# A fourth buffer for the scan's states, and the next sequence's softplus in the buffer of u

## The chip, the cores and the metric

The kernel runs on one core of one Trainium2 chip. The metric is the device time of one execution in microseconds. The engines are called by their names in the profile: PE (TensorE, matmuls), PEld (its weight loads), DVE (VectorE), ACT (ScalarE), POOL (GpSimd), SP (SyncE, whose queue issues the DMAs named here). Each engine runs its own instructions strictly in order.

## What is computed

The input is x, 16 sequences of 512 tokens with 256 features, float32. Four residual layers follow one another:

```
x = x + mamba(layernorm(x))         # the state-space scan: the part that changes here
x = x + ffn(layernorm(x))           # "f": weights and activations rounded to FP4 in blocks of 16
x = x + linear_attention(layernorm(x))
x = x + ffn(layernorm(x))           # "g": the same weights
```

The scan layer, with 16 states per feature:

```
x_in = x @ w_in                                   # u
dt   = softplus(x_in @ w_x[:, :64] @ w_dt + b_dt) * 0.099 + 0.001
B, C = columns 64..79 and 80..95 of x_in @ w_x
bar  = exp(dt * A),  A = -exp(A_log)
h    = bar * h + inp,   inp[n] = B[n] * sum_d dt[d] A[d, n] u[d]
y    = sum_n h[:, n] C[n] + D * u
```

## The kernel before

All 16 sequences pass through four stages: scan, ffn "f", attention, ffn "g". The stages of different sequences overlap: `run_all` holds a generator for each stage with a begin and a length in units of a sequence's scan, and always advances the one that is furthest behind. A generator yields estimated costs between its pieces. From this the program text is emitted in one interleaved order, and the tile framework's scheduler then arranges each engine's instructions. The resulting order on each engine is fixed before the kernel runs. Stage b of the scan begins at b, of "f" at b+1, of attention at b+2.1, of "g" at b+3.1, so in the middle of the run four sequences are in flight.

A sequence's scan (`mamba`) has 16 steps, one for each (e, j, q0), a tile of 128 rows (16 states times 8 features) by 2x512 times:

1. `spread` (L520) copies rows of softplus's result from the DRAM tile `dd` to one of four decay tiles `bars`, each feature row to its 16 state rows. It can be issued when the scan that used this tile four steps earlier has ended.
2. `decay` (L527, L530) turns it into the decay: two Exp on ACT and one Square.
3. L548 is the scan on DVE, h = bar * h + inp, over 1024 columns. L552 multiplies by C (`cm`).
4. Two steps make a pair: L558 on PE sums the 16 states of both into `py`.

`h` has the tag "hs" with three buffers, so a scan has to wait until the py matmul three scans earlier has read its tile. `py` begins with the product of D's diagonal and u (L544); the second of a sequence's two py tiles begins at step 9, where `halfway` is set. After the eighth and the sixteenth step py goes through L565 (yT), transposes (L568) and L571 into the residual x.

The scan of sequence b+1 needs a `prologue` (L449), which is woven between the steps of scan b:

- `front` (L435): layer norm statistics and the transposed, scaled input tT_m;
- pz (L457), softplus's argument, on PE; L466 and L467 on ACT take its absolute value and its ReLU; L471 and L472 are Tanh and Ln with a table load; L473 on DVE joins them to dt;
- eight DMAs (L478) that write dt to `dd`;
- pcm and its copy cm (L483);
- a guard, which holds the generator until scan b has passed its half; it is needed because u has one buffer and u of sequence b is read by the second L544;
- pu and its two copies to u (L490), L493 (dt times u, DVE), pg and pbm on PE (L496, L457), L501 (ACT), L502 (DVE), which gives `term`.

The next `mamba` then copies `term` to the two halves of `inp` (L510 on ACT, L511 on POOL), which has one buffer, so these wait for the sixteenth scan of the sequence before; then its first scan can start.

The other names in the prediction: in an ffn, `hidden(c)` runs pg and pu (L605), Tanh (L611), two products on DVE (L612, L613), and the FP4 rounding (L230 to L252, with one ACT step L248, big); `down(c)` runs transposes pt_h (L627), copies hqT (L631, L636), the matmul po (L640) and the residual (L377 or L647). In the attention, `scores` makes psc (L722) and the masked sm (L729), and `attend` makes pn (L745, L753), pr, pk, pkv, and yT (L773); pro (L800) is its projection. `h_g_3` means chunk 3 (of 0 to 3) of "g", and so on. PSUM has seven banks for all of these and one for py.

Of the kernel before, what the change touches and what calls it, by code (L numbers as in the profile page):

```python
# [10 lines left out]
F32 = mybir.dt.float32  # L11
# [6 lines left out]
P = 128  # L18
# [14 lines left out]
def kernel(  # L33
# [19 lines left out]
    B, S, D = x.shape  # L53
# [6 lines left out]
    ND = D // P  # L60
# [18 lines left out]
    def bank(name):  # L79
        return ps.tile([P, 512], F32, tag="bank", name=name)  # L80
# [7 lines left out]
    one = ctx.enter_context(tc.tile_pool(name="one", bufs=1))  # L88
# [8 lines left out]
    begun, turned, stats, halfway = {}, {}, {}, [0]  # L97
# [270 lines left out]
    def summed(i, name):  # L368

        sums = small.tile([P, NC], F32, tag=f"sum{i}", name=f"sum_{name}")  # L370
        dist = small.tile([P, NC], F32, tag=f"dist{i}", name=f"dist_{name}")
        return sums, dist
# [10 lines left out]
    def distances(xt, c, sums, dist):  # L383
        nc.scalar.activation(
            squares, xt[:, c, :], AF.Square, bias=sums[:, c : c + 1], scale=-float(D),
            accum_out=dist[:, c : c + 1],
        )
# [47 lines left out]
    def front(b, xt):  # L435

        stats = small.tile(
            [P, NC, nc.vector.BN_STATS_DIM], F32, tag="stats", name=f"st_m{b}"
        )
        mv = small.tile([P, NC, nc.vector.BN_AGGR_DIM], F32, tag="mv", name=f"mv_m{b}")  # L440
        for c in range(NC):
            nc.vector.bn_stats(stats[:, c, :], xt[:, c, :])
            nc.vector.bn_aggr(mv[:, c, :], stats[:, c, :])
        rstd = inverse(2, mv[:, :, 1], 1.0, f"m{b}")
        yield 2.4
        turned[b] = to_features(one, xt, f"m{b}", rstd)
        yield 1

    def prologue(b, xt):  # L449

        yield from front(b, xt)
        xnT = turned.pop(b)

        def from_xn(w, name):
            p = bank(f"{name}_{b}")
            for k in range(ND):
                nc.tensor.matmul(p, w[:, k], xnT[:, k, :], start=(k == 0), stop=(k == ND - 1))  # L457
            return p

        soft = one.tile([P, ND, S], F32, tag="soft", name=f"soft_{b}")
        dt = one.tile([P, ND, S], F32, tag="dt", name=f"dt_{b}")
        for e in range(ND):
            pz = from_xn(w_z_sb[:, :, ts(e, P)], f"pz{e}")
            nc.scalar.activation(soft[:, e, :], pz, AF.Abs, bias=b_dt_sb[:, e : e + 1])  # L466
            nc.scalar.activation(  # L467
                dt[:, e, :], pz, AF.Relu, bias=b_relu[:, e : e + 1], scale=DT_MAX - DT_MIN
            )
        yield 0.5  # L470
        nc.scalar.activation(soft, soft, AF.Tanh, scale=0.5)  # L471
        nc.scalar.activation(soft, soft, AF.Ln, bias=half_c, scale=0.5 * LN_C)  # L472
        nc.vector.scalar_tensor_tensor(dt, soft, DT_MIN - DT_MAX, dt, ALU.mult, ALU.add)  # L473

        dd = dram.tile([ND, 2, 32, 2, S], F32, tag="dt", name=f"dd_{b}")
        for e in range(ND):
            for q in range(4):
                nc.sync.dma_start(  # L478
                    dd[e, q // 2, :, q % 2, :], dt[32 * q : 32 * q + 32, e, :]
                )  # L480
        yield 1.5
        cm = one.tile([P, S], F32, tag="cm", name=f"cm_{b}", bufs=2)
        nc.scalar.copy(cm, from_xn(w_c_sb, "pcm"))  # L483
        yield 0.1

        while halfway[0] < b:
            yield 0
        u = one.tile([P, ND, S], F32, tag="u", name=f"u_{b}")
        for e in range(ND):
            nc.scalar.copy(u[:, e, :], from_xn(w_in_sb[:, :, ts(e, P)], f"pu{e}"))  # L490
        yield 0.5

        nc.vector.tensor_tensor(dt, dt, u, ALU.mult)  # L493
        pg = bank(f"pg_{b}")
        for k in range(ND):
            nc.tensor.matmul(  # L496
                pg, a_rep[:, k].rearrange("p n i -> p (n i)"), dt[:, k, :],
                start=(k == 0), stop=(k == ND - 1),
            )
        term = dt[:, 0, :]  # L500
        nc.scalar.copy(term, from_xn(w_b_sb, "pbm"))  # L501
        nc.vector.tensor_tensor(term, term, pg, ALU.mult)  # L502
        begun[b] = (u, dd, term, cm)
        yield 2

    def mamba(b, xt):
        u, dd, term, cm = begun.pop(b)

        inp = one.tile([P, 2, S], F32, tag="inp", name=f"inp_{b}")
        nc.scalar.copy(inp[:, 0, :], term)  # L510
        nc.gpsimd.tensor_copy(inp[:, 1, :], term)  # L511

        halves = small.tile([P, ND, NC], F32, tag="halves", name=f"halves_{b}")

        def spread(e, j, q0):

            bar = bars[state["bar"] % NBAR]
            state["bar"] += 1
            src = dd[e, q0 // 2, j * G8 : (j + 1) * G8, :, 1:S]
            nc.sync.dma_start(bar[:, :, 1:S], src.unsqueeze(0).to_broadcast([NS, G8, 2, S - 1]))  # L520
            return bar

        def decay(bar, e, j, q0):

            for i in range(2):
                g = 16 * e + 4 * (q0 + i) + j
                nc.scalar.activation(  # L527
                    bar[:, i, 1:S], bar[:, i, 1:S], AF.Exp, scale=a_col[:, g : g + 1]
                )
            nc.scalar.activation(bar[:, :, 1:S], bar[:, :, 1:S], AF.Square)  # L530
            return bar

        steps = [(e, j, q0) for e in range(ND) for j in range(4) for q0 in (0, 2)]
        sps = [spread(*steps[at]) for at in range(NBAR - 1)]
        ahead = decay(sps[0], *steps[0])
        for at, (e, j, q0) in enumerate(steps):
            bar = ahead
            if at + 1 < len(steps):
                ahead = decay(sps[at + 1], *steps[at + 1])
            if at + NBAR - 1 < len(steps):  # L540
                sps.append(spread(*steps[at + NBAR - 1]))
            if j == 0 and q0 == 0:
                py = ps_y.tile([P, S], F32, tag="y", name=f"py_{b}_{e}")
                nc.tensor.matmul(py, d_diag[:, e], u[:, e, :], start=True, stop=False)  # L544
                if e == ND - 1:
                    halfway[0] = b + 1
            h = one.tile([P, 2, S], F32, tag="hs", name=f"h_{b}_{e}_{j}_{q0}", bufs=3)
            nc.vector.tensor_tensor_scan(  # L548
                h.rearrange("p i t -> p (i t)"), bar.rearrange("p i t -> p (i t)"),
                inp.rearrange("p i t -> p (i t)"), 0.0, ALU.mult, ALU.add,  # L550
            )
            nc.vector.tensor_tensor(h, h, cm.unsqueeze(1).to_broadcast([P, 2, S]), ALU.mult)  # L552
            if q0 == 0:
                h0 = h
            else:

                for q in range(4):
                    nc.tensor.matmul(  # L558
                        py[32 * q : 32 * q + 32, :], red[:, j, :], (h0, h)[q // 2][:, q % 2, :],
                        start=False, stop=(j == 3),  # L560
                    )
            if j == 3 and q0 == 2:

                yT = one.tile([P, S], F32, tag="yT", name=f"yT_{b}_{e}")
                nc.scalar.copy(yT, py)  # L565
                pt = bank(f"pt_y_{b}_{e}")
                for c in range(NC):
                    nc.tensor.transpose(pt[:, ts(c, P)], yT[:, ts(c, P)], ident)  # L568
                for c in range(NC):
                    xc = xt[:, c, ts(e, P)]  # L570
                    nc.vector.scalar_tensor_tensor(  # L571
                        xc, pt[:, ts(c, P)], 1.0, xc, ALU.mult, ALU.add,
                        accum_out=halves[:, e, c : c + 1],
                    )
            yield 3.5

        stats["f", b] = sums, dist = summed(0, f"f{b}")
        nc.vector.tensor_tensor(sums, halves[:, 0, :], halves[:, 1, :], ALU.add)
        for c in range(NC):
            distances(xt, c, sums, dist)  # L580
        yield 2
# [268 lines left out]
    def scan(b):  # L850

        if b + 1 < B:
            xs.append(load(b + 1))
            yield from weave(mamba(b, xs[b]), prologue(b + 1, xs[b + 1]), 1)
        else:
            yield from mamba(b, xs[b])
# [76 lines left out]
```

## Time and profile before

| | us |
|---|---|
| three runs, median (lowest to highest) | 2812.1 (2811.1 to 2816.2) |
| profiled execution, its own time | 2810.3 |
| its span, first to last instruction | 2808.6 |
| PE busy | 2443.9 |
| DVE busy | 2432.7 |
| ACT busy | 1491.0 |
| POOL busy | 171.8 |
| mean granted PE clock | 0.944 of full |

The span is the time from the first to the last instruction on the core. A busy time is the sum of an engine's instructions without the overlap of consecutive ones. A row of the costliest groups gives line, engine, operation, output and inputs, the number of instructions, their total and mean time, and how long the engine was idle just before them, with what ended that. In the answers on waits the three numbers are the total in us, how often, and the longest. In a timeline the two numbers ahead are the start in us from the span's start and the duration; the bracket holds the idle time before and its cause.

Single rows used later: L511 on POOL takes 0.61 to 1.60 us, median 1.46; L478 issues in 0.42 us (median) and lands 1.7 us after; a spread (511 KB) lands 4.7 us after its issue; an ACT table load takes 1.28 us, and there are 33.

### The profile page before, as it was taken

The numbers are of one execution on the slowest core, as the hardware profiler recorded it, in microseconds if no ns is written. First come the engines' busy times: TensorE is split into PE (matmuls) and PEld (weight loads), VectorE is DVE, ScalarE is ACT, GpSimd is POOL, SyncE is SP. The second block draws the span as 40 slices with busy tenths as digits, with TensorE's granted clock in tenths as the row PEclk, the third lists the DMA queues.
The fourth block names the chain that finished last, engine by engine and source line by source line (L and its number), as shares of the span: only waits on it lengthen the run. The fifth ranks groups of instructions, "written<-read, shape, count | busy, mean of one in ns | idle before, by whom it ended". The sixth has DMA issues, their size and how long they took to land.

```text
span 2808.6 us, 34278 instructions
## 1 busy us (share of the span) xinstructions
PE 2443.9 (87%) x12907; PEld 1436.5 (51%) x12907; DVE 2432.7 (87%) x3689; ACT 1491.0 (53%) x2846; POOL 171.8 (6%) x171
## 2 busy tenths in 40 slices
PE   5677889799888898989889898989989898899996
PEld 3234545455555555555555555555555555455664
DVE  7898888898899889989989989898899988987665
ACT  4766564465636456464555646455564645433321
POOL 2000000000001000000100000010000001000000
PEclk7788999999999999999999999999999999999998
DMA  5433212223113131311313222131321312200000
GB/s 141 128 97 83 67 46 53 68 53 83 53 38 83 38 90 38 90 46 38 84 44 79 49 61 74 38 75 45 83 53 51 85 37 69 53 1 8 8 1 15
DMA packets 97146, 165.01 MB, mean 59 GB/s; under 512 B 8434, under 2 KB 92372, under 8 KB 96980
## 3 DMA queue, kind: packets, MB, share of 16 engines
q1 hardware_dynamic: 95360, 161.77, 22.5%
q8 instruction: 101, 1.65, 0.3%
q10 hardware_dynamic: 1620, 1.06, 0.1%
q14 instruction: 65, 0.53, 0.1%
HBM read 146.02 MB, written 16.78 MB: 58 GB/s over the span
## 4 chain that ended last, share of the span: by engine, by line
DVE 40%; PE 35%; DMA 10%; ACT 9%; issue 4%; POOL 2%; SPq 0%; POOLq 0%; ACTq 0%; DVEq 0%
DVE h L548 15%; DMA bar<-dd 10%; PE pg_g L605 5%; DVE h L552 4%; PE pu_g L605 4%; PE po_g L640 3%; PE pg_f L605 3%; PE pu_f L605 3%; PE py L558 3%; ACT bar L527 2%; DVE sm L729 2%; PE pz L457 2%; DVE v_f L244 1%; ACT bar L530 1%; PE po_f L640 1%
## 5 line engine op out<-in xcount | busy, mean ns | idle before, releaser
L548 DVE TENSOR_TENSOR_SCAN h<-bar,inp 128x1024 f32<-128x1024 f32 x256 | 579.6, 2278 | 12.1 <-PE py L558 5.9
L527 ACT ACTIVATE bar<-bar,a_col 128x511 f32<-128x511 f32 x512 | 352.4, 716 | 358.5 <-DMA bar<-dd 305.8
L558 PE MATMUL py<-h,red 128*32 128x512 f32 x1024 | 289.6, 649 | 122.5 <-DVE h L552 121.7
L552 DVE TENSOR_TENSOR h<-h,cm 128x1024 f32<-128x1024 f32 x256 | 311.3, 1218 | 0.6
L530 ACT ACTIVATE bar<-bar 128x1022 f32<-128x1022 f32 x256 | 269.3, 1052 | 3.0
L640 PE MATMUL po_g<-wdT,hqT_g 128*128 128x256 f32 (+1 forms) x768 | 205.9, 412 | 40.2 <-ACT hqT_g L631 40.2
L640 PE MATMUL po_f<-wdT,hqT_f 128*128 128x256 f32 (+1 forms) x768 | 197.9, 400 | 9.5 <-ACT hqT_f L631 8.3
L640 PEld LDWEIGHTS po_g<-wdT,hqT_g 128*128 128x128 f32 (+1 forms) x768 | 143.7, 199 | 113.7 <-ACT hqT_g L631 64.2
L605 PE MATMUL pg_g<-wgT,tT_g 128*128 128x352 f32 x512 | 194.1, 500 | 0.2 <-ACT tT_g L419 0.2
L605 PE MATMUL pu_g<-wuT,tT_g 128*128 128x352 f32 x512 | 185.6, 487 | 0.0
L640 PEld LDWEIGHTS po_f<-wdT,hqT_f 128*128 128x128 f32 (+1 forms) x768 | 137.0, 191 | 95.0 <-ACT hqT_f L636 29.9
L605 PE MATMUL pg_f<-wgT,tT_f 128*128 128x352 f32 x512 | 182.0, 479 | 0.1
L605 PE MATMUL pu_f<-wuT,tT_f 128*128 128x352 f32 x512 | 172.9, 460 | 3.3 <-DVE sm L729 3.3
L729 DVE TENSOR_TENSOR sm<-psc,causal 128x512 f32<-128x512 f32 x256 | 164.1, 680 | 2.2 <-PE pn L753 1.3
L611 ACT ACTIVATE h_g<-pg_g 128x352 f32<-128x352 f32 x128 | 59.1, 462 | 199.9 <-PE pg_g L605 199.9
L558 PEld LDWEIGHTS py<-h,red 128*32 128x32 f32 x1024 | 37.9, 111 | 224.9 <-DVE h L552 173.9
L605 PEld LDWEIGHTS pu_g<-wuT,tT_g 128*128 128x128 f32 x512 | 105.1, 206 | 64.1 <-issue 14.8
L612 DVE SCALAR_TENSOR_TENSOR h_g<-h_g,pg_g 128x352 f32<-128x352 f32 x128 | 65.6, 512 | 79.9 <-ACT h_g L611 78.7
L763 POOL COPY dx<-den 128x256 f32<-128x256 f32 x64 | 42.7, 667 | 1455.7 <-PE pr L768 776.7
L605 PEld LDWEIGHTS pg_f<-wgT,tT_f 128*128 128x128 f32 x512 | 95.4, 195 | 67.4 <-issue 22.8
L678 PE MATMUL pqk<-tT_a,w_qkv_sb 128*128 128x512 f32 x256 | 121.2, 610 | 7.2 <-ACT tT_a L430 7.2
L605 PEld LDWEIGHTS pu_f<-wuT,tT_f 128*128 128x128 f32 x512 | 97.1, 190 | 58.9 <-DVE sm L729 5.2
(237 smaller groups left out, 4674.1 us busy)
## 6 DMA issues: line engine op xcount, KB each, us to landing
bar<-dd SPq DMA_DIRECT2D x256, 511.0 KB, 4.7
x<-in_L_attn_a_x_dram SPq DMA_DIRECT2D x16, 512.0 KB, 4.5
dd<-dt SPq DMA_DIRECT2D x128, 64.0 KB, 1.7
out_dram<-x SPq DMA_DIRECT2D x16, 512.0 KB, 4.9
w_qkv_sb<-in_L_attn_b_W_attn_dram ACTq DMA_DIRECT2D x1, 768.0 KB, 7.3
raw_d<-in_L_ffn_w_down_dram SPq DMA_DIRECT2D x1, 704.0 KB
raw_g<-in_L_ffn_w_gate_dram SPq DMA_DIRECT2D x1, 640.0 KB, 7.1
raw_u<-in_L_ffn_w_up_dram SPq DMA_DIRECT2D x1, 640.0 KB, 6.3
```

The source lines that it names most:

```text
L457: nc.tensor.matmul(p, w[:, k], xnT[:, k, :], start=(k == 0), stop=(k == ND - 1))
L527: nc.scalar.activation(bar[:, i, 1:S], bar[:, i, 1:S], AF.Exp, scale=a_col[:, g : g + 1])
L530: nc.scalar.activation(bar[:, :, 1:S], bar[:, :, 1:S], AF.Square)
L548: nc.vector.tensor_tensor_scan(h.rearrange("p i t -> p (i t)"), bar.rearrange("p i t -> p (i t)"), inp.rearrange("p i t -> p (i t)"), 0.0, ...
L552: nc.vector.tensor_tensor(h, h, cm.unsqueeze(1).to_broadcast([P, 2, S]), ALU.mult)
L558: nc.tensor.matmul(py[32 * q : 32 * q + 32, :], red[:, j, :], (h0, h)[q // 2][:, q % 2, :], start=False, stop=(j == 3),)
L605: nc.tensor.matmul(pw[:, :HF], xqT[:, k, ts(c, P)], wT[:, k, cols], start=(k == 0), stop=(k == ND - 1),)
L611: nc.scalar.activation(hc, pg[:, :HF], AF.Tanh, scale=0.5)
L612: nc.vector.scalar_tensor_tensor(hc, hc, 1.0, pg[:, :HF], ALU.add, ALU.mult)
L640: nc.tensor.matmul(po[:, :D], hqT[:rows, r, :], wdT[:rows, r, :], start=(r == 0), stop=(r == NR - 1),)
L678: nc.tensor.matmul(pz, w_qkv_sb[:, k, ts(je, P)], xnT[:, k, :], start=(k == 0), stop=(k == ND - 1),)
L729: nc.vector.tensor_tensor(t, psc[g].rearrange("p (s t) -> p s t", t=P), causal.unsqueeze(1).to_broadcast([P, NH // 4, P]), ALU.mult,)
```

## The change

The prologue's softplus result `soft` no longer has a buffer of its own: it takes the one of u (tag "u"). The guard moves from before u to before `soft`, since the buffer is free only when scan b has read its own u for the last time. So pz, softplus, the writes to `dd` and cm are issued after the half of scan b, as u was already. The 4 KB per partition that soft held go to a fourth buffer for the states h.

```diff
@@ prologue
+        while halfway[0] < b:
+            yield 0
+
-        soft = one.tile([P, ND, S], F32, tag="soft", name=f"soft_{b}")
+        soft = one.tile([P, ND, S], F32, tag="u", name=f"soft_{b}")
         dt = one.tile([P, ND, S], F32, tag="dt", name=f"dt_{b}")
...
         nc.scalar.copy(cm, from_xn(w_c_sb, "pcm"))
         yield 0.1
-
-        while halfway[0] < b:
-            yield 0
         u = one.tile([P, ND, S], F32, tag="u", name=f"u_{b}")
@@ mamba
-            h = one.tile([P, 2, S], F32, tag="hs", name=f"h_{b}_{e}_{j}_{q0}", bufs=3)
+            h = one.tile([P, 2, S], F32, tag="hs", name=f"h_{b}_{e}_{j}_{q0}", bufs=4)
```

In the changed kernel the lines below the guard's new place are three higher as far as cm (L473 becomes L476); from u on (L490) they are the same.

## The prediction

> **What bounds the kernel now.** I read the page's first part, then the chain, then who VectorE (DVE) waits for, all of it and in one sequence, and last the timelines of that sequence.
>
> ```profile
> span 2808.6 us, 34278 instructions
> PE 2443.9 (87%) x12907; PEld 1436.5 (51%) x12907; DVE 2432.7 (87%) x3689; ACT 1491.0 (53%) x2846; POOL 171.8 (6%) x171
> DVE 40%; PE 35%; DMA 10%; ACT 9%; issue 4%; POOL 2%; SPq 0%; POOLq 0%; ACTq 0%; DVEq 0%
> L548 DVE TENSOR_TENSOR_SCAN h<-bar,inp 128x1024 f32<-128x1024 f32 x256 | 579.6, 2278 | 12.1 <-PE py L558 5.9
> ```
>
> DVE and TensorE (PE) are both near full and share the chain, so the instruction order, above all DVE's, sets the time. A sequence takes about 165.4 us where all stages overlap. The scan rows waited for a py matmul, which frees a state buffer, only 5.9 us in the whole run. Where DVE does wait, in one sequence (1255.0 to 1420.4 us):
>
> ```profile
> DVE h_g L612 <- ACT h_g L611: 6.4, 3, 5.2
> DVE h_f L612 <- ACT h_f L611: 3.6, 2, 3.3
> DVE v_g L250 <- ACT big_g L248: 2.6, 2, 2.0
> DVE yT L773 <- ACT num L760: 1.1, 1, 1.1
> DVE kv L789 <- PE pkv L784: 0.6, 1, 0.6
> DVE dt L493 <- ACT u L490: 0.4, 1, 0.4
> ```
>
> All its waits sum to 16.3 us, so DVE works 149.1 of 165.4 us. Three gaps hold most of it:
>
> ```profile
> 1255.38 3.60 PE L457 MATMUL pz<-tT_m,w_z_sb 128*128 128x512 f32 x8
> 1261.61 0.52 DVE L612 SCALAR_TENSOR_TENSOR h_g<-h_g,pg_g 128x352 f32<-128x352 f32 x1 [5.25 <-ACT h_g L611]
> 1324.47 0.89 DVE L250 SCALAR_TENSOR_TENSOR v_g<-big_g,v_g 128x704 f32<-128x704 bf16 x1 [1.98 <-ACT big_g L248]
> 1364.58 0.52 DVE L612 SCALAR_TENSOR_TENSOR h_f<-h_f,pg_f 128x352 f32<-128x352 f32 x1 [3.35 <-ACT h_f L611]
> ```
>
> Gap A, 5.25 us: PE runs the next sequence's pz ahead of a gate product that DVE wants, and ScalarE (ACT) runs softplus ahead of its tanh. Gap B, 3.35 us: ACT stands in exps of decay tiles that have not landed, and a tanh is queued behind.
>
> **The change part by part.** No operation is added or removed; SBUF is equal (soft's 4 KB per partition pay for the fourth h). Both programs load ACT's tables 33 times. All that moves is order and two waits. I number a sequence's scans 1 to 16 and take DVE's order from the built programs where all stages overlap.
>
> *Does the prologue move?* Yes: L473 (after: L476) stood between scans 9 and 10, and now between 14 and 15; L493 from before scan 11 to after 16; L502 from before scan 14 to directly ahead of the next scan 1.
>
> *Fourth state buffer.* DVE's order now holds scans 1 to 4 in one bunch (before: 1 to 3). A rule speaks for a large gain: the Trainium skill, "Perfetto Trace Analysis", Optimization Strategy, says that a gap which repeats on the engine that should be full can mean too few buffers for the next tile. By it the 16.3 us would be the prize, 15 x 16.3 = 240 us. The row above says that state buffers held DVE for 5.9 us in all. I take the row: gain 0 to 6 us, taken as 3.
>
> *Soft in u's buffer.* Soft must wait for u's last reader (L544), u(b+1) for L476. The guard in the generator already puts soft behind the first, and L490 comes some 20 us after L476. Cost 0.
>
> *Gap A.* pz now follows psc_1 on PE. From there to the next gate product PE has pz 3.6, py, po_g, about 10 us; DVE has about 16 us of work: masks, h_f_1's quantization, scans 13 and 14, L476. Hidden, gain 5.25. *Gap B.* Scans 5 to 8's exps now come between the two tanhs of h_f_3; by landing 4.6 us after scans 1 to 4, the first tanh ends 10.8 us after scan 1 starts, the second 15.7, where DVE reaches them at 12.7 and 16.1. Gain 3.35. The 1.98 gap and the two waits of 1.1 and 0.6 (attention, now with DVE behind PE) go too: together 12.3 of 16.3. The small rest, 4.0, I keep.
>
> *The dd writes.* Eight issues, 0.42 us each, now stand in SP's queue behind scan 16's spread and ahead of the next scan 1's; SP waits there for L476 and the next four spreads are queued behind. L476 + 3.7 (issue) + 1.7 (landing) + 4.7 (spread) = 10.1 us; ACT comes to that exp 10.6 us after L476 (behind h_f_2's tanh). Cost 0, up to 2 if late.
>
> *The end of the sequence*, where I see the price. The rows for it:
>
> ```profile
> 1340.25 1.33 ACT L527 ACTIVATE bar<-bar,a_col 128x511 f32<-128x511 f32 x2 [2.87 <-DMA bar<-dd]
> 1338.61 3.05 PE L640 MATMUL po_g<-wdT,hqT_g 128*128 128x256 f32 x12
> 1290.56 3.70 PE L457 MATMUL pu<-tT_m,w_in_sb 128*128 128x512 f32 x8
> 1320.28 1.98 PE L496 MATMUL pg<-dt,a_rep 128*128 128x512 f32 x4
> 1322.11 1.88 PE L457 MATMUL pbm<-tT_m,w_b_sb 128*128 128x512 f32 x4
> 62.49 2.29 DVE L548 TENSOR_TENSOR_SCAN h<-bar,inp 128x1024 f32<-128x1024 f32 x1 [1.09 <-ACT inp L510]
> ```
>
> Count from scan 16's end. It frees the last decay tile for next scan 4. Before, such an exp started 4.6 us after its scan (a scan ended at 1335.6, the exp came at 1340.25). In ACT's new order exp 1.3, square 1.0, cm 0.5 follow, and only then the copies hqT_g_2 (0.65): 8.1. PE, start to start: po_g_2 3.0, pt_h_g_3 0.8, wait for hqT_g_3 1.2, po_g_3 3.0, pu 3.6: done at 20.1. ACT's u copy: L493 starts at 21.0. PE goes on, pn_1 2.0, pr and pk 0.5, pkv with its identity part 1.15, D's diagonal product 0.9, pro_1 1.7, pg 1.83, pbm 1.71: 29.9. L501 0.7, L502 0.75: 31.3. The copies to inp cost the 1.09 of the last row, where scan 1 also stood right behind L502: 32.4. DVE's own work from scan 16 to the next scan 1 is 17.3 us by the starts of the same rows, so it idles 15.1: about 1 on v_f, 4.6 on po_g_3, 4.0 on u, 1 on pro_1, 3.5 on L501, 1.1 on inp. Before, L493 and L502 lay among other work and scan 16 to scan 1 had no gap.
>
> On that last term a second rule: "GPSIMD Engine Reference", Specifications, has GpSimd (POOL) share its SBUF interfaces with VectorE, with contention from DVE instructions of two SBUF inputs. The trace's POOL copy takes 0.61 us at the start, with DVE idle, against a median of 1.46. Read by the rule, a waiting DVE lets the copy be short, 1.09; by the median it would be 1.9, 0.8 x 15 = 12 us more. I take 1.09, as DVE will be idle, and keep 12 for the range.
>
> *Sum.* After: 15.1 + 4.0 = 19.1 idle per sequence against 16.3, so +2.8 where all stages overlap, about 11 sequences: +31. In the first four transitions gaps A and B are smaller (fewer stages), the L493 to scan 1 chain is the same but has less PE work in it: about +3.7 each (2.6 on pg and pbm, 1.1 on inp), +15. Less 3 for the buffer: +43. The profiled execution took 2810.3 us (span 2808.6 and 1.7 around it), 1.8 under the median of 2812.1 us. From the median: 2855.
>
> **The rivals.**
>
> *Faster.* If ACT is not late with hqT_g_2 (the exps of next scans 1 to 4 done 3.5 us earlier, since PE is free then), the end costs 11.6, and if the dense rest loses its small waits too (4.0 to 1.0), a sequence idles 12.6: -3.7, x 15 = -55: about 2757. For it: gaps A and B alone are 8.6. Against it: PE's own row sum from po_g_2 to pbm is 21 us, and no order in DVE's list puts other work into it.
>
> *Much slower.* Scan 1 is late, so the four decay tiles that scans 1 to 4 free in one bunch are late, and ACT, in order, waits at them (it already waits 305.8 us for such landings) with tanhs behind. It decides once ACT reaches the second tanh over 0.4 us later than I have it; 4 us more per sequence x 15 = +60: about 2915.
>
> *No change.* The end costs 12.3, exactly what goes elsewhere: 2812.
>
> **How the numbers follow.** Slower as summed 0.55, much slower 0.15, no change 0.06, faster 0.24. About 0.2% is what a measurement of this kernel can tell from no change. Predicted 2855. The first case alone has 2830 to 2880 (1.5 us per sequence either way). The range takes in part of both other sides: 2780 to 2905. Faster 0.24, same 0.06, slower 0.70.
>
> **What would show it.** In the profile after: the wait of h_g L612 for its tanh falls from 78.7 to near 25 us and h_f's from 70.5 to near 35; dt L493 for u rises from 9.7 to 40 or more; dt L502 for L501 from 2.7 to 40 or more; x L647 for po_g from 32.5 to 80 or more; scan L548 gets a wait for inp of some 15. Busy time of DVE stays at 2433. I am wrong if L493 and L502 show almost no wait (the end is then covered), or if A stays.

## The result and the profile after

The changed kernel is slower, by less than half of what was forecast.

| | before | after |
|---|---|---|
| median of five runs each, us | 2812.1 (2803.4 to 2816.2) | 2825.2 (2822.8 to 2828.3) |
| ratio, 95% interval | | 1.0049 (1.003 to 1.0069) |
| span of the profiled execution, us | 2808.6 | 2822.8 |
| DVE busy, us | 2432.7 | 2413.3 |
| DVE idle (span less busy), us | 375.9 | 409.5 |
| mean granted PE clock | 0.944 | 0.929 |

The page after, with the same lines as were shown of before: head, busy times, chain by engine, and the row of the scans.

```profile
span 2822.8 us, 34208 instructions
PE 2430.3 (86%) x12907; PEld 1453.7 (51%) x12907; DVE 2413.3 (85%) x3689; ACT 1491.6 (53%) x2846; POOL 167.7 (6%) x171
PE 37%; DVE 31%; ACT 14%; DMA 10%; issue 4%; POOL 3%; SPq 0%; POOLq 0%; ACTq 0%; DVEq 0%
L548 DVE TENSOR_TENSOR_SCAN h<-bar,inp 128x1024 f32<-128x1024 f32 x256 | 579.7, 2276 | 15.5 <-POOL inp L511 9.8 <-ACT bar L530 3.3 <-ACT inp L510 2.4
```

DVE's share of the chain falls from 40% to 31%, PE's and ACT's rise: the end of a sequence is now a chain through them. But DVE also has 19.4 us *less* busy time with the same 3689 instructions. No step of the prediction had that. Now DVE's waits after, over the whole run (total us, times, longest):

```profile
DVE x L647 <- PE po_g L640: 91.7, 41, 7.1
DVE dt L502 <- ACT dt L501: 50.2, 15, 5.6
DVE dt L493 <- ACT u L490: 45.9, 12, 3.8
DVE h_g L612 <- ACT h_g L611: 21.6, 22, 4.9
DVE h_f L612 <- ACT h_f L611: 20.8, 26, 3.6
DVE h L548 <- POOL inp L511: 9.8, 13, 0.8
```

These are the moves that were forecast: the waits for a tanh (78.7 and 70.5 us before) are mostly gone, and the three waits at the end of a sequence (32.5, 2.7 and 9.7 before) have taken their place. ACT's wait for landing decay tiles fell from 305.8 to 182.5 us. The timeline of one sequence's end, on DVE and then on PE:

```profile
1321.35 2.29 DVE L548 TENSOR_TENSOR_SCAN h<-bar,inp 128x1024 f32<-128x1024 f32 x1
1341.11 0.42 DVE L647 TENSOR_TENSOR x<-x,po_g 128x256 f32<-128x256 f32 x1 [4.35 <-PE po_g L640]
1345.36 1.23 DVE L493 TENSOR_TENSOR dt<-dt,u 128x1024 f32<-128x1024 f32 x1 [3.83 <-ACT u L490]
1354.59 0.69 DVE L502 TENSOR_TENSOR dt<-dt,pg 128x512 f32<-128x512 f32 x1 [3.45 <-ACT dt L501]
1356.03 4.47 DVE L548 TENSOR_TENSOR_SCAN h<-bar,inp 128x1024 f32<-128x1024 f32 x2 [0.75 <-POOL inp L511]
```

```profile
1331.56 4.74 PE L640 MATMUL po_g<-wdT,hqT_g 128*128 128x256 f32 x12 [2.13 <-ACT hqT_g L631]
1338.02 3.05 PE L640 MATMUL po_g<-wdT,hqT_g 128*128 128x256 f32 x12
1341.00 3.70 PE L457 MATMUL pu<-tT_m,w_in_sb 128*128 128x512 f32 x8
1350.23 1.98 PE L496 MATMUL pg<-dt,a_rep 128*128 128x512 f32 x4
1352.05 1.88 PE L457 MATMUL pbm<-tT_m,w_b_sb 128*128 128x512 f32 x4
```

Scan 16 ends at 1323.64. From there L493 starts 21.7 us later (forecast 21.0), L502 31.0 (30.6), and the next scan 1 32.4 (32.4). DVE's waits in one sequence, 1355.3 to 1522.9 us, sum to 19.5 us (forecast 19.1). So the end of the sequence came out as long as forecast (how far by luck is said below), and the missing 29 us are elsewhere. Cutting the run at the starts of the first scans shows where. The rows are: stretch, its length, then busy time and instructions of PE, PEld, DVE, ACT, POOL, and PE's clock, the DMA share, GB/s; first of before, then of after, each from the fifth sequence's first scan to the sixteenth's:

```profile
517.97:2344.05 1826.08, 1641.59 (x8816) 966.06 (x8812) 1639.31 (x2509) 1013.80 (x1936) 112.21 (x99) 0.97 0.24 61
```

```profile
513.80:2359.67 1845.87, 1632.38 (x8824) 983.32 (x8823) 1623.73 (x2499) 1013.67 (x1936) 102.58 (x98) 0.95 0.24 60
```

These eleven sequences take 19.8 us longer. DVE's idle time rises by 35.4 (1826.1 less 1639.3 is 186.8; 1845.9 less 1623.7 is 222.1), its work falls by 15.6. The idle time has two parts. The waits that the profile lists rise from 174 to 217 us, by 43; gaps too short for that list fall by 8. The four sequences ahead of the eleven take 451.4 us instead of 455.5, and what lies around both takes 1.5 less: 19.8 - 4.1 - 1.5 = 14.2, the difference of the spans.

### The profile page after: what moved, and what is told of

Read it like the earlier page. It is cut to its first block, busy times and chain, and to the rows that moved or that the text cites. A ratio compares the mean times of both kernels' runs of the same rounds, so it can differ in the third digit from the quotient of the medians.

```text
span 2822.8 us, 34208 instructions
## 1 busy us (share of the span) xinstructions
PE 2430.3 (86%) x12907; PEld 1453.7 (51%) x12907; DVE 2413.3 (85%) x3689; ACT 1491.6 (53%) x2846; POOL 167.7 (6%) x171
## 4 chain that ended last, share of the span: by engine, by line
PE 37%; DVE 31%; ACT 14%; DMA 10%; issue 4%; POOL 3%; SPq 0%; POOLq 0%; ACTq 0%; DVEq 0%
DVE h L548 12%; DMA bar<-dd 10%; PE po_g L640 7%; ACT bar L527 3%; DVE h L552 3%; PE py L558 3%; PE pg_g L605 2%; ACT bar L530 2%; PE pu_g L605 2%; PE pu_f L605 2%; PE pz L457 2%; PE pu L457 2%; PE pn L753 1%; PE pg L496 1%; PE pt_h_g L627 1%
## 5 line engine op out<-in xcount | busy, mean ns | idle before, releaser
L527 ACT ACTIVATE bar<-bar,a_col 128x511 f32<-128x511 f32 x512 | 348.3, 714 | 220.9 <-DMA bar<-dd 182.5
L558 PE MATMUL py<-h,red 128*32 128x512 f32 x1024 | 238.4, 640 | 40.3 <-DVE h L552 40.3
L605 PE MATMUL pu_f<-wuT,tT_f 128*128 128x352 f32 x512 | 194.1, 505 | 82.1 <-DVE sm L729 43.6
L640 PE MATMUL po_g<-wdT,hqT_g 128*128 128x256 f32 (+1 forms) x768 | 218.3, 431 | 39.9 <-ACT hqT_g L631 39.9
L640 PEld LDWEIGHTS po_g<-wdT,hqT_g 128*128 128x128 f32 (+1 forms) x768 | 150.4, 209 | 120.0 <-ACT hqT_g L631 55.9
L605 PE MATMUL pg_g<-wgT,tT_g 128*128 128x352 f32 x512 | 183.8, 481 | 4.1 <-DVE sm L729 3.9
L605 PE MATMUL pu_g<-wuT,tT_g 128*128 128x352 f32 x512 | 176.5, 463 | 0.4 <-DVE sm L729 0.4
L763 POOL COPY dx<-den 128x256 f32<-128x256 f32 x64 | 31.1, 485 | 1949.8 <-PE pr L768 1296.1
L426 PE MATMUL pt_a<-diag_a,x 128*128 128x128 f32 x256 | 57.7, 410 | 81.5 <-ACT diag_a L424 81.4
L605 PEld LDWEIGHTS pu_g<-wuT,tT_g 128*128 128x128 f32 x512 | 97.0, 192 | 54.9 <-issue 1.8
L605 PEld LDWEIGHTS pg_g<-wgT,tT_g 128*128 128x128 f32 x512 | 91.6, 193 | 59.0 <-DVE sm L729 10.8
```

Of the source, the lines that this page charges most:

```text
L426: nc.tensor.matmul(pts[k][:, ts(c, P)], t[:, c, ts(k, P)], diag, start=True, stop=True)
L527: nc.scalar.activation(bar[:, i, 1:S], bar[:, i, 1:S], AF.Exp, scale=a_col[:, g : g + 1])
L558: nc.tensor.matmul(py[32 * q : 32 * q + 32, :], red[:, j, :], (h0, h)[q // 2][:, q % 2, :], start=False, stop=(j == 3),)
L605: nc.tensor.matmul(pw[:, :HF], xqT[:, k, ts(c, P)], wT[:, k, cols], start=(k == 0), stop=(k == ND - 1),)
L640: nc.tensor.matmul(po[:, :D], hqT[:rows, r, :], wdT[:rows, r, :], start=(r == 0), stop=(r == NR - 1),)
```

## The experiments

Ratios are to the kernel before, timed beside each run; after's is 1.0049.

**The end of the sequence: is it exposed?** The same edit in both kernels makes pbm twice, so that PE has some 1.7 us more per sequence, between pg and L501.

```diff
-        nc.scalar.copy(term, from_xn(w_b_sb, "pbm"))
+        pbm = bank(f"pbm_{b}")
+        for k in (0, 1, 0, 1):
+            nc.tensor.matmul(pbm, w_b_sb[:, k], xnT[:, k, :], start=(k == 0), stop=(k == 1))
+        nc.scalar.copy(term, pbm)
```

In the kernel after:

> The changed kernel with the matmuls of pbm done twice into the same bank (the result is the second). Theory 1: PE's chain from scan 16 to the next scan 1 sets DVE's start, so the whole 1.71 us is paid 15 times: +22 to +28 us over the changed kernel, and the wait of L502 for L501 grows from 50 to about 75 us. Rival (the loss is spread over the sequence, or comes from the lower granted clock): +0 to +10.

In the kernel before:

> The same doubling in the kernel before, where pbm and L502 lie among other work. Theory 1: mostly hidden, 0 to +10 us. Rival: the same amount as in the changed kernel.

Measured: after 2849.9 us, ratio 1.0172 (1.0154 to 1.019), so some 34 us more than after has (1.0172 less 1.0049, of 2803); before 2821.4, ratio 1.0065 (1.005 to 1.008), 18 us more. Both cost more than expected, and after's more than before's. The lines on L502's wait, of after with the edit and then of before with it (three lines further down in the program):

```profile
DVE dt L505 <- ACT dt L504: 78.2, 16, 5.5
```

```profile
DVE dt L505 <- ACT dt L504: 6.3, 3, 3.5
```

In after, 28 of the 34 us stand in this one wait (50.2 before the edit), so what PE does there is on the path and DVE has nothing to put beside it. In before the wait grows by 3.6 only, and the 18 us are spread over others: h_f's wait for its tanh, for one, goes from 70.5 to 84.8. So before was not as free there as was expected: the same work costs it half as much as after.

**The fourth buffer, alone and with the move.** First the move without the buffer: the diff's prologue part, with `bufs=3` for h.

> The change without the fourth state buffer: soft in u's buffer, guard moved, three buffers for h. Theory 1 (the lateness of the prologue is what costs: after scan 16 a chain hqT_g_2, po_g_2, po_g_3, pu, u, L493, pg, pbm, L501, L502, inp runs while DVE has half as much work): the waits of L647 for po_g, L493 for u and L502 for L501 together stay above 120 us (before 44.7, after 187.8), time 2825 to 2850. Rival (the fourth buffer's bunch of scans 1 to 4 makes the end late): these waits fall to near 45, time 2805 to 2815. Theory 2 (DVE's own work fell in the change because fewer instructions stand directly behind the one whose output they read: 444 such neighbours before, 299 after, 19.4 us less busy): here the order has 387, so DVE busy near 2425.

Measured: 2939.3 us, ratio 1.0491 (1.0473 to 1.0508); DVE busy 2427.3, idle 508.5. The time misses by 89 us. The end-of-sequence waits are there as expected (40.3, 52.6 and 77.0), but others have come back:

```profile
DVE dt L493 <- ACT u L490: 77.0, 12, 8.0
DVE h_f L612 <- ACT h_f L611: 72.5, 36, 4.5
DVE qk L686 <- ACT ep L685: 71.7, 21, 5.7
DVE h L548 <- PE py L558: 26.0, 24, 1.4
```

Given the moved prologue, the fourth buffer is worth 4%, about 120 us, and only 26 us of that is a wait for a state buffer. The rest stands in waits that have nothing to do with a state buffer: with three buffers the program is laid out in another order (L476 stands behind scan 12, and behind scan 14 in after).

Then the buffer without the move. It needs memory, which here comes from the attention's masked scores (`NSM`, L67, their number of buffers); the second kernel is the control, with that edit alone.

```diff
-    NSM = 6
+    NSM = 4
...
-            h = one.tile([P, 2, S], F32, tag="hs", name=f"h_{b}_{e}_{j}_{q0}", bufs=3)
+            h = one.tile([P, 2, S], F32, tag="hs", name=f"h_{b}_{e}_{j}_{q0}", bufs=4)
```

> The kernel before with a fourth state buffer and no change of the prologue; the 4 KB come from the attention's masked scores, four buffers instead of six. The order of DVE then has all of the prologue's DVE work behind scan 16 (L473, L493 and L502), with 52 us of other work beside it. Theory 1 (what costs is a late prologue, however it comes to be late): L502's wait and the decay tiles' landing for scan 1 to 4 are on the path; time 2830 to 2900. Rival (the fourth buffer is a gain in itself, as e1 against the changed kernel suggests): 2760 to 2803.

> The kernel before with NSM = 4 in place of 6 and still three state buffers: the control of the run with the fourth buffer alone, which took its memory from NSM. DVE's order here has L473 and L493 after scan 13 and L502 after scan 16. Theory 1 (a late prologue with three buffers is dear, as in the moved prologue with three buffers, and the fourth buffer is what makes it bearable): 2860 to 2940, slower than the run with four buffers (ratio 1.021). Rival (the fourth buffer alone pulled the prologue late and is to blame for that run's 2%): 2795 to 2830, as before.

Measured: with four buffers 2858.4 us, ratio 1.0209 (1.019 to 1.0228); the control, with three, 2871.4, ratio 1.0249 (1.0234 to 1.0265). So taking two score buffers away costs the 2%, and on top of it the fourth state buffer gains 0.4%, about 11 us; the two ratios come from different chips, each to before beside it. Both orders have a late prologue, though the guard is where before has it: L502 stands behind scan 16 in both, L473 and L493 behind scan 16 with four buffers and behind scan 13 with three. What a fourth buffer is worth in the order of before itself, with six score buffers, was not measured. One buffer is worth 11 us between one pair of orders and 120 between another. Its price can't be read from one row of waits.

**Soft in a state buffer.** Four buffers for h, soft in one of them (tag "hs"), and the guard where before has it: a way to have the buffer without the late prologue.

> The fourth state buffer without the wait for u: soft takes one of the four h buffers in rotation, the guard stays where it was before. Theory 1: the prologue's pz, softplus and dd writes are early again (L473 after scan 7, L493 after scan 13), so the wait of L493 for u is below 20 us and L647's for po_g below 60; L502 still stands after scan 16, so some of its 50 us stay. Time 2795 to 2820. Rival (the fourth buffer costs): 2825 or more. Theory 2: 437 neighbours, DVE busy near 2432.

Measured: 3024.2 us, ratio 1.079 (1.0774 to 1.0806), over 200 us above what was expected; DVE busy is 2442.1, 10 above. L493's wait is 1.6 us and L502's 24.1, so the end of the sequence is shorter as meant, but DVE idles 576.1 us, with po_f (84.6), po_g (57.8) and ep (60.1) in front, at a PE clock of 0.889. What of this is soft's hold on a state buffer and what is the new order was not separated; it is no way to a better kernel.

**What took 19.4 us from DVE's work.** In the program, an instruction that reads or overwrites what an earlier DVE instruction wrote waits for that instruction's semaphore (the signal of its end), on the same engine. Where the earlier one stands directly ahead, the two can't overlap. Rows of after show it, first two products on different tiles, then a chain on one tile (v_f, each behind its own producer):

```profile
1324.77 0.89 DVE L251 SCALAR_TENSOR_TENSOR v_g<-big_g,v_g 128x704 f32<-128x704 bf16 x1
1325.57 0.52 DVE L613 SCALAR_TENSOR_TENSOR h_f<-h_f,pu_f 128x352 f32<-128x352 f32 x1
...
1332.54 0.89 DVE L250 SCALAR_TENSOR_TENSOR v_f<-big_f,v_f 128x704 f32<-128x704 bf16 x1 [1.17 <-ACT big_f L248]
1333.46 0.89 DVE L251 SCALAR_TENSOR_TENSOR v_f<-big_f,v_f 128x704 f32<-128x704 bf16 x1
1334.39 0.89 DVE L252 TENSOR_TENSOR h_f<-v_f,half_f 128x704 f32<-128x704 f32 x1
```

From start to start the unrelated pair takes 0.80 us, the chain 0.92 and 0.93, though each first instruction lasts the same 0.89. Two small kernels measure it alone. The first has chains of one instruction kind, on one tile and on two in turn:

```python
for _ in range(64): op(ta)                  # each behind its own producer
for _ in range(32): op(tb); op(te)          # one other instruction between
# the same with 704 columns: wa; wb, we
```

> Not the reference's computation: it copies x to the output and, beside that, runs four chains of 64 equal scalar_tensor_tensor instructions on DVE: 352 columns, each on the output of the one just before it; 352 columns, two tiles in turn, so that each works on the output of the one before last; then both with 704 columns. Theory 2 (an instruction right behind the one whose output it reads starts later): from the fit over six profiles, DVE busy = 2347.6 + 0.129 x neighbours + 0.092 x waits, the step from start to start is 0.10 to 0.16 us longer in the first and third chain than in the second and fourth, the same for both widths. Rival (the saving came from something else): steps equal within 0.03.

Measured, from the timeline: 352 columns, 35.79 us for 64 on one tile (0.559 each) against 0.436 in turn; 704 columns, 59.30 for 64 (0.927) against 0.80. The difference is 0.12 to 0.13 us, whatever the width. But is it the data or the wait? The next two runs change one operand of L613, so that it no longer reads what L612 wrote but still overwrites it. The order on DVE stays the same.

```diff
-                nc.vector.scalar_tensor_tensor(hc, hc, 0.5, pu[:, :HF], ALU.mult, ALU.mult)
+                nc.vector.scalar_tensor_tensor(hc, wgT[:, 0, cols], 0.5, pu[:, :HF], ALU.mult, ALU.mult)
```

In the kernel before:

> The kernel before, with one operand changed: the second product of an ffn's hidden layer (L613) takes a constant (rows of wgT, same shape) in place of h, so it no longer depends on the product before it (L612). The output is therefore not the reference's; operations, shapes and DVE's order are those of before. In that order L613 stands directly behind its own L612 88 times. Theory 1 (an instruction directly behind its producer costs DVE 0.12 us more): DVE busy falls from 2432.7 by 88 x 0.12 = 10.6 to about 2422, the time by 5 to 11 us. Rival (the difference in DVE's busy time came from waits or from what else lies beside the work): busy stays within 2 us of 2432.7.

In the kernel after:

> The same operand changed in the kernel after (again not the reference's output); there L613 stands directly behind its own L612 only 44 times. Theory 1: DVE busy falls from 2413.3 by 44 x 0.12 = 5.3 to about 2408, half of what the same edit takes off before; the gap between the two kernels' busy times shrinks from 19.4 to about 14. Rival: no change in busy, and the gap stays at 19.

Measured: ratios 0.9999 (0.9987 to 1.0011) and 1.0071 (1.0058 to 1.0085), the latter with after's own 1.0049 (1.003 to 1.0069) overlapping. The busy lines, before with the edit and after with it:

```profile
PE 2441.9 (87%) x12907; PEld 1438.1 (51%) x12907; DVE 2433.5 (87%) x3689; ACT 1490.1 (53%) x2846; POOL 170.6 (6%) x171
```

```profile
PE 2433.6 (86%) x12907; PEld 1455.6 (52%) x12907; DVE 2413.7 (86%) x3689; ACT 1491.4 (53%) x2846; POOL 167.5 (6%) x171
```

2433.5 and 2413.7: nothing moved, and theory 1 as worded there is refuted. L613 still waits for L612's semaphore, because it writes the same tile. That gave theory 1a, the wait itself, and the second small kernel:

```python
for _ in range(64): op(aa, aa)                              # reads and overwrites
for _ in range(64): op(bb, kb)                              # only overwrites
for _ in range(32): op(ca, kc); op(cb, kc)                  # two tiles in turn
for _ in range(32): op(dd[:, :352], kh); op(dd[:, 352:], kh)  # two halves in turn
```

> A small kernel of its own (it copies x to the output and computes none of the reference): four chains of 64 VectorE instructions of one kind (scalar_tensor_tensor, 128x352), one after the other. aa: each reads and writes the same tile. bb: each writes the same tile and reads a constant, so no data passes between neighbours, but the program still makes each wait until the one before has finished. ca, cb: two tiles written in turn from a constant, each waits for the one before the last. dd: the two halves of one tile in turn, waits as for ca, cb. Theory 1a (the wait for the instruction directly ahead costs 0.12 us, whatever passes between them; this is why changing an operand of L613 left DVE's busy time alone): start to start aa 0.56, bb 0.56, ca/cb 0.44, dd 0.44 us. Rival 1b (reading what was just written costs it): aa 0.56, bb, ca/cb and dd 0.44 us.

Its timeline on DVE:

```profile
1.26 35.76 DVE L68 SCALAR_TENSOR_TENSOR aa<-aa 128x352 f32<-128x352 f32 x64
37.05 0.34 DVE L72 COPY kb<-aa 128x352 f32<-128x352 f32 x1
37.43 35.76 DVE L68 SCALAR_TENSOR_TENSOR bb<-kb 128x352 f32<-128x352 f32 x64
73.22 0.34 DVE L75 COPY kc<-bb 128x352 f32<-128x352 f32 x1
73.60 0.53 DVE L68 SCALAR_TENSOR_TENSOR ca<-kc 128x352 f32<-128x352 f32 x1
...
101.59 0.52 DVE L79 TENSOR_TENSOR kh<-ca,cb 128x352 f32<-128x352 f32 x1
102.15 27.96 DVE L68 SCALAR_TENSOR_TENSOR dd<-kh 128x352 f32<-128x352 f32 x64
```

64 of aa and 64 of bb take 35.79 us each (0.559 us), ca and cb 27.99 (0.437), dd 27.96 (0.437). No data passes in bb, and it pays the same: the wait for the instruction directly ahead costs 0.122 us, reading costs nothing more. The instructions in turn wait too, for the one before the last, and pay nothing. One thing is not separated: bb also overwrites the addresses that the instruction ahead wrote, and a wait between instructions that share none was not tried.

Of the 0.122 us, 0.09 is lost overlap, which counts as busy time: an instruction lasts 0.52 to 0.53 us, and in turn the next starts 0.44 after it. The other 0.03 is a gap behind its end, which counts as idle.

Counted in the two programs, 359 DVE instructions of before wait for the one directly ahead, 202 of after. The profiles agree: each of them starts at least 0.033 us after the end of the one ahead, while of the others, those with a listed wait left out, the median starts 0.08 us before it. At 0.122 us the 157 fewer are 19 us. Measured are 19.4 us less work and some 9 us less of short gaps (idle less the listed waits: 24 us before, 15 after), 29 in all. So the waits for the one directly ahead make up two thirds; the rest was not traced. Over the twelve full kernels here (before, after and ten runs) a fit gives DVE busy = 2361.5 + 0.116 us for each such wait + 0.098 for each of the waits for others that the profile lists, and is off by 3.7 us at most, where the busy times differ by 29. The edit of L613 leaves the count at 359 and 202, which is why it did nothing. No run changes the count of a full kernel and leaves its order alone.

**Another pace for "g".** Two more orders of the kernel after, through the length given to stage "g" (L894, 0.6 in both kernels):

```diff
-        times = [(b, 1.0), (b + 1.0, 1.0), (b + 2.1, 0.9), (b + 3.1, 0.6)]
+        times = [(b, 1.0), (b + 1.0, 1.0), (b + 2.1, 0.9), (b + 3.1, 0.7)]
```

> The changed kernel with a stage length of 0.7 in place of 0.6 for the last ffn, so that the order changes: between scan 16 and the next scan 1 po_g_3 stands behind L493 and not ahead of it, and pu is behind one po_g instead of two. DVE's work there is 17.7 us (changed: 19.4 by the same count), 287 neighbours. Theory 1: L647's wait falls from 91.7 to below 60 and L493's below 30, time 2795 to 2815 where before is 2803. Rival (any order that begins the prologue in the second half costs about the same): L647, L493 and L502 together stay near 188, time 2815 to 2830.

And with 0.5 in that place:

> The changed kernel with a stage length of 0.5 for the last ffn: all of po_g_2 and po_g_3 are then placed away from the end of the sequence, where pu, pg and pbm stay; 304 neighbours. Theory 1: the wait for po_g at the end is gone (L647 below 50), L493 and L502 keep 40 to 90 together, time 2790 to 2815 where before is 2803. Rival: 2815 to 2830.

Measured: 2872.4 us, ratio 1.025 (1.022 to 1.0281), and 2826.1, ratio 1.0102 (1.0063 to 1.0141). Both miss. With 0.5 the end of the sequence got lighter: L493's wait fell from 45.9 to 1.7 us, L647's from 91.7 to 43.0. Yet DVE's idle time is 406.4 us against 409.5, since tanh and the residual of "f" are waited for instead, and L502 as before:

```profile
DVE h_f L612 <- ACT h_f L611: 67.5, 49, 4.0
DVE x L377 <- PE po_f L640: 54.1, 17, 4.4
DVE dt L502 <- ACT dt L501: 54.1, 15, 3.8
```

With 0.7 L493's wait for u is gone, but L647's is 70.0 where below 60 was expected, the two tanh waits come back (46.3 and 43.8), and idle is 439.1. None of the runs on the full computation beats before.

## Why the prediction was right in sign and wrong in size

**The term that failed: "No operation is added or removed ... All that moves is order and two waits", and from it "Busy time of DVE stays at 2433".** It fell to 2413.3. Order alone changes DVE's work, since 157 fewer of its instructions wait for their direct predecessor. In the eleven sequences that is 15.6 us of work and 8 us of short gaps, where the sum had nothing. That such a wait costs 0.122 us is shown by the second small kernel and by the two runs that changed the data and not the wait; what it comes to in the full kernels is count times price, two thirds of what was measured. Why the new order divides more chains was not examined.

**The second term: the first four transitions, "about +3.7 each, +15".** Measured: -4.1 in all, of it -0.9 idle and -3.2 work. The priced chain is there (L502's wait goes from 1.0 to 12.0 us), but h_f's falls from 13.3 to 6.0, the scan's for a state buffer from 4.2 to nothing, and other small ones go as well. "Gaps A and B are smaller" was taken as no gain at all. The move without the fourth buffer takes 452.7 us for the same four (before 455.5, after 451.4), so most of this gain belongs to the moved prologue, as far as one profile of each can tell. Which part of the move brings it was not tried.

**The end of the sequence and the gaps: right in the total, with luck in it.** L493, L502 and the next scan 1 came within 0.7 us of the forecast, and the tanh waits of gaps A and B fell by 96 us in the eleven sequences, where 8.6 each, 95, were forecast (over the run they stand at 21.6 and 20.8; near 25 and 35 were forecast). L493, L502 and L647 passed 40, 40 and 80 us as forecast. The 1.98 gap on v_g was to go: v_g's waits fell from 24.9 to 18.5 us only. In all, a sequence's listed waits went from 15.8 to 19.8 us on average, where the sum had 16.3, from the one sequence that was read, and 19.1.

The luck: po_g_2 was put at 3.0 us of PE and took 4.7: PE had just waited 2.13 us for hqT_g_2, and its granted clock was 0.64 there (the last three columns are PE's clock, the DMA share, GB/s):

```profile
1331.50:1336.30 4.80, 4.74 (x13) 3.17 (x14) 2.67 (x3) 1.00 (x4) 0.00 (x0) 0.64 0.01 3
```

Smaller slips the other way hid this: the terms up to pu add to 19.7, not to the 20.1 that was written; pn_1 to pro_1 took 5.7 us where 6.25 were put; inp cost 0.75, not 1.09. In nine of the eleven ends po_g_2 takes 4.5 to 4.7 us. In the other two it takes 3.05 at full clock; in the one shown PE waits as long ahead of it:

```profile
1166.44 3.05 PE L640 MATMUL po_g<-wdT,hqT_g 128*128 128x256 f32 x12 [2.12 <-ACT hqT_g L631]
```

There the next scan 1 comes 30.7 and 30.9 us after scan 16, where the nine have 32.4 to 34.3. At 1.7 us for each of the nine the lower clock is worth some 15 us, an estimate from these rows; no run tested it, nor what the lower mean clock (0.95 against 0.97 in the eleven) costs elsewhere. No step of the prediction had the clock. The scan's wait for inp is 12.2 us over the run, with 15 forecast.

**The POOL copy: the right choice, by more than it assumed.** The sum took 1.09 us for inp and kept the median, 1.46, as the dear end. The wait is 0.75, and L511 takes 716 ns on average (median 612) where it took 1311 (1461). By the median the forecast would have been 12 us worse still. The direction is that of the rule on shared interfaces; no run separates that from what else differs between the kernels.

**The fourth buffer, "0 to 6, taken as 3": wrong as a price.** Given the move, taking it away costs about 120 us. It did not spoil this sum, because the order that was walked already held the four buffers. But as a statement on the buffer the row of 5.9 us said nearly nothing: it tells what the order of before waits for, not which order three or four buffers lead to. The rule that a repeating gap can mean too few buffers, read as 240 us, was not borne out either: with the guard where it was and two score buffers fewer, the fourth buffer gains 11 us.

Put together: 31 + 15 - 3 = 43 was forecast, all of it idle time. Measured, DVE's listed waits rise by 43 over the run, which agrees by luck (the eleven +43 where +31 was forecast, the first four about -1 where +15 was), and its work and short gaps fall by 29, for which the sum had nothing: 43 - 29 is the +14 that was measured. The rival *faster* had the end of the sequence cheaper than it is (12.6 us idle against 19.5); *much slower* had ACT late with the bunched exps, and the tanh waits say that it is not.

## What to carry to other kernels

When only order changes, an engine's busy time is not a constant: count in both programs how many of its instructions wait for the one directly ahead on the same engine, and price the difference (0.122 us each on this DVE). A chain walked engine by engine from the built order gave the length of the new end within half a microsecond, but single terms were off by up to 1.7 us: compare the terms too, and look at the granted clock where PE starts again after a wait. Do the same walk for the start of the run, not a scaled guess. A buffer's worth lies in the order that it permits, so it is measured by removing it in the new order, not read from a wait in the old one.

## What was not expected of the hardware

- A DVE instruction that waits for the one directly ahead starts 0.122 us later than one that waits for the instruction before that (0.559 against 0.437 us from start to start at 128x352), and it does not matter whether data passes. The Trainium skill, "VectorE: DVE Perf Modes", The DRAIN you can't avoid, finds for eight tensor_copy that a semaphore after each costs nothing extra; for the instructions measured here it does when it is waited for at once, and one instruction between hides it. The same section says that a read of what was just written needs the semaphore or one DVE instruction between, so the wait is to be hidden, not left out.
- PE's granted clock was 0.64 over po_g_2 at the end of a sequence, and its twelve matmuls took 4.74 us; at full clock, after a wait as long, they took 3.05.
- POOL's copy of 128x512 float32 takes 0.72 us on average in after, where DVE mostly waits for it, and 1.31 us in before, where DVE is mostly at work beside it.
